# A four-layer RWKV and graph-conv network on one core: the first pair's sums on VectorE, the last layer norm ahead of a gelu, the last conv in another order of chunks

## The chip, the core and the metric

The kernel runs on one core of a Trainium2 chip. A core has TensorE (PE, matmuls into PSUM; PEld is its weight load), VectorE (DVE), ScalarE (ACT), GpSimd (POOL) and SyncE (SP, which here only issues DMAs). Each engine works through its own instruction queue in order; semaphores tie the queues together. The metric is the device time of one execution in microseconds (us), lower is better.

## What is computed

The input `x` is 16 images of 192 channels by 56 x 56. Three layers mix along the 3136 pixels with a two-way RWKV scan, a fourth is a graph conv. Each adds to its input, and each normalises its input first over groups of 6 channels and all pixels:

```python
xs = tokens(_gn(x))                       # layers 0 to 2; _gn: group norm, 32 groups
k, v, r = xs @ Wk.T, xs @ Wv.T, xs @ Wr.T
h = sigmoid(r) * 0.5 * (wkv_scan(k, v) + flip(wkv_scan(flip(k), flip(v))))
h = (h - mean(h)) * rsqrt(var(h) + eps) * ln_g + ln_b     # layer norm over channels
x = x + h @ Wo.T

g = _gn(x)                                # layer 3
x_j = max(roll(g, 2, rows), roll(g, -2, rows), roll(g, 2, cols), roll(g, -2, cols), g) - g
y = conv_w @ concat(g, x_j) + conv_b      # then batch norm
x = x + gelu(y)
```

## The kernel before

The images are worked two at a time, so there are eight *pairs*. A pair's 192 channels of two images fill three tiles of 128 partitions (`ORDER` = 0, 2, 1; tile 1 holds the upper 64 channels of both). The pixels are cut into `NL` = 7 *chunks* of `L` = 448. A *run* is one layer of one pair (`l` = 0 to 2 the scans, `l` = 3 the conv). A run's forward scan goes over chunks 0 to 6 (`"A"` units), its backward scan, gate, layer norm and output over chunks 6 to 0 (`"B"` units); a conv run has one `"C"` unit per chunk. `"Z"` units only load a pair's input so that its sums and squares can be counted.

The instructions of each engine are laid down by hand, in the order in which the Python code calls them, inside `manual_schedule`. Two streams of pairs interleave: while one pair is in its backward scan, the other is in a forward scan or a conv. A list `steps` pairs them up. Its first seven steps are the forward scan of pair 0 alone. Its last steps are: the backward scan of pair 7's third layer beside the conv of pair 6, the last conv chunk of pair 6 alone (`forward_c`), an empty step (`neither`), and the conv of pair 7, chunks 0 to 6, alone (`forward_c`).

The work around the change:

- **Statistics.** `chunk_stats` (L734, L735) takes a sum (Identity with accumulation) and a sum of squares per tile and chunk on ScalarE. For pair 0 all seven chunks are counted at the very start (L1708, L1709); at the same time the layer parameters are prepared outside the hand-made order (`layer_params`), and a scheduler mixes the two on each queue.
- **Group norm.** `norm_sums` (L740), `norm_var` (L749 to L765) and `norm_fold` (L777 to L784, L770) turn the sums into a scale that is folded into the layer's weights. They are called one part at a time through `gap()`. A group's mean rides as an extra column (`mean_column`, L765) behind chunk 0. The run's weights are loaded by `begin_later`, once the last chunk's new statistics are taken (`b_stats`).
- **Layer norm of a B unit.** After `b_mix` (L1031 to L1033, GpSimd) come `b_squares` (L1040, ScalarE), `b_sums` (L1047, L1049, TensorE), `b_rs1` to `b_rs3` (L1055, L1059, L1063, L1065), `b_spread` (L1071), `b_scale` (L1076), `b_out` (ops) and `b_x` (L1089 and the store to `xd`). `late` notes how far a unit has come. In the empty step `finish` brings the last units through.
- **Conv of a chunk.** `c_product` half 0 multiplies x (TensorE, "cv<-x"); `c_rows` (L1114 to L1116) and `c_columns` (L1125 to L1129) form the maxima on VectorE, from the chunk and two rows of its neighbours on each side, the *ring* `m<-xd`; `c_product` half 1 multiplies the maxima ("cv<-m"); `c_gelu` (L1150) reads PSUM on ScalarE; `c_add` (L1159) adds x on GpSimd for all three tiles at once; `store` (L1178 to L1181) issues four DMAs one step later.
- **Last of all**, outside the hand-made order, L1755 to L1759 reduce the accumulated checks to a flag, which decides whether a general version of the whole network is run after this one.

Of the kernel before, what the change touches and what calls it, by code (L numbers as in the profile page):

```python
# [473 lines left out]
def fast_path(ctx: ExitStack, tc: tile.TileContext, flag, x, wproj, wfold, wcfold, wconst, wgroup, sums, picks, vecs, out):  # L474
# [63 lines left out]
    def column(j):  # L538
        return slice(j % 2, j % 2 + 1)
# [172 lines left out]
    class Run:  # L712
        def __init__(self, pr, l, stats, src=None, first=None):
            self.pr, self.l, self.stats, self.src = pr, l, stats, src
            self.xa, self.xb, self.xz = {}, {}, {}
            if first is not None:
                self.xa[0] = first
            self.begun, self.before = False, None
            self.bias, self.ps = {}, {}
            self.ek, self.ekv, self.h, self.den, self.sg, self.rs = {}, {}, {}, {}, {}, {}  # L720
            self.m, self.ml, self.q, self.p = {}, {}, {}, {}
            self.done = set()
# [23 lines left out]
    def norm_var(run):  # L746
        m = run.ps["g"][:, 0:6].rearrange("p (j s) -> p j s", s=2)
        nm = run.nm = stile("nm")
        V.tensor_scalar(nm, m[:, :, 0:1], -1.0 / T, None, ALU.mult)  # L749
        m2 = stile("m2")  # L750
        V.tensor_mul(m2, nm, nm)
        var = run.var = stile("var")
        V.scalar_tensor_tensor(var, m[:, :, 1:2], 1.0 / T, m2, ALU.mult, ALU.subtract)
        release(run.ps.pop("g"))
        V.tensor_scalar(var, var, EPS, None, ALU.add)
        rstd = run.rstd = stile("rstd")
        S.activation(rstd, var, AF.Ln)
        S.activation(rstd, rstd, AF.Exp, scale=-0.5)
        run.chk = small.tile([P, NCHK], F32, tag="chk", name=name("chk"))
        mean_check = run.chk[:, 3 * NL + 9 : NCHK].rearrange("p (j o) -> p j o", o=1)  # L760
        V.scalar_tensor_tensor(mean_check, var, -MEAN_MAX, m2, ALU.mult, ALU.add)
        mean_column(run, run.xa[0])

    def mean_column(run, s):
        V.tensor_copy(s.full[:, :, L : L + 1], run.nm)  # L765
# [44 lines left out]
    def load_weights(run):  # L810
        kv = wpool.tile([P, 2, FCOLS], F32, tag="kv", name=name("wkv"))
        if run.l == NLAYERS:
            nc.sync.dma_start(kv, wcfold)
            run.weights = kv, None
        else:
            nc.sync.dma_start(kv, wfold[run.l, :, 0:2, :])
            r = wpool.tile([P, 1, FCOLS], F32, tag="r", name=name("wr"))
            nc.sync.dma_start(r, wfold[run.l, :, 2:3, :])
            run.weights = kv, r
        load_ahead(("C" if run.l == NLAYERS else "A", run, 0))  # L820

    def gap(eng=V):
        if norms:
# [11 lines left out]
    def load_ahead(unit):  # L835

        if unit is None:
            return
        kind, run, c = unit
        chunks = {"A": run.xa, "C": run.xa, "B": run.xb, "Z": run.xz}[kind]  # L840
        if c not in chunks and (kind, c) != ("B", NL - 1):
            chunks[c] = load_chunk(run, c)
        if kind == "C" and c not in run.xb:
# [264 lines left out]
    def c_rows(run, c):  # L1108
        xt, m = run.xa[c].t, run.xb.pop(c)
        run.m[c] = m  # L1110
        E = L - SHIFT
        if c == 0:
            mean_column(run, m)
        V.tensor_max(m.t[:, :, SHIFT:E], xt[:, :, 0 : E - SHIFT], xt[:, :, 2 * SHIFT : L])  # L1114
        V.tensor_max(m.t[:, :, 0:SHIFT], m.t[:, :, 0:SHIFT], xt[:, :, SHIFT : 2 * SHIFT])
        V.tensor_max(m.t[:, :, E:L], xt[:, :, E - SHIFT : E], m.t[:, :, E:L])  # L1116

    def c_columns(run, c):
# [9 lines left out]
        V.tensor_max(ml.t, ml.t, xt)  # L1128
        V.tensor_max(m, m, ml.t)  # L1129

    def c_product(run, c, half):
        n = L + 1 if c == 0 else L
        if half == 0:
            run.ps["c"] = banks("cv")
        s = (run.xa if half == 0 else run.m)[c]
        project(run.ps["c"], run.w[half], lambda rows, j: s.full[rows, j, 0:n], n, half == 0, half == 1)
        if half == 1:
            run.m.pop(c).give()

    def c_gelu(run, c, more):  # L1140
        g, ps = run.ml[c], run.ps["c"]
        if c == 0:
            run.bias["c"] = stile("cvb")
            for j in ORDER:
                V.tensor_scalar(
                    run.bias["c"][:, j, :], ps[j][:, L : L + 1], conv_inv[:, column(j)], conv_bias[:, column(j)],
                    ALU.mult, ALU.add,
                )
        for j in ORDER:
            S.activation(  # L1150
                g.t[:, j, :], ps[j][:, 0:L], AF.Gelu, bias=run.bias["c"][:, j, :], scale=conv_inv[:, column(j)]
            )
            release(ps[j])
        if not more:
            S.preload_act_table_set(TABLES)
# [9 lines left out]
    def c_end(run, c, more):  # L1165
        c_gelu(run, c, more)
        c_add(run, c)


    stores = []  # L1170
# [23 lines left out]
    for pr in range(npairs):  # L1194
        runs = [Run(pr, 0, None)]
        for l in range(NLAYERS):
            runs[-1].follow = Run(pr, l + 1, None)
            runs[-1].follow.before = runs[-1]
            runs[-1].dst = [dram.tile([P, 3, L], F32, tag=f"x{pr}_{l}_{c}", name=name("xd")) for c in range(NL)]
            runs.append(runs[-1].follow)  # L1200
        chains.append(runs)

# [9 lines left out]
    while ready[turn] is not None:  # L1212
        run, other = ready[turn], 1 - turn
        units = []
        ready[other] = None
        while todo[other]:
            r = todo[other].pop(0)
            units += front(r)
            if r.l < NLAYERS:
                ready[other] = r  # L1220
                break
        if len(units) > NL:

            units[NL - 1], units[NL] = units[NL], units[NL - 1]
        steps.append([("B", run, NL - 1), None, []])
        for c in reversed(range(NL - 1)):
            steps.append([("B", run, c), units.pop(0) if units else None, []])
        steps += [[None, u, []] for u in units]
        if len(streams) == 1 or ready[other] is None:

            units = []
            while todo[turn]:
                r = todo[turn].pop(0)
                units += front(r)
                if r.l < NLAYERS:
                    ready[turn] = r
                    break
            else:
                ready[turn] = None
            steps += [[None, None, []]] + [[None, u, []] for u in units]  # L1240
        else:
            turn = other
# [358 lines left out]
            keys(nkeys)  # L1601
            exp_keys(nkeys)

    def forward_c(a, nback, nfront):
        h = of_stage(0.5)
        load_ahead(nback)
        ahead = nfront is not None and nfront[1].begun
# [2 lines left out]
        if h and ahead and nfront[0] == "A":  # L1610
            c_rows(*a)
            b_rs2(*h)
            b_rs3(*h)
            sum_up(1)
            c_columns(*a)
            store()
            b_spread(*h)
            keys(nfront)
            exp_keys(nfront)
            b_scale(*h)  # L1620
            a_q(*nfront[1:])
            a_save(*nfront[1:])
            a_values(*nfront[1:])
            b_out(*h)
            late[h] = 2
            convs.extend(((a, 0), (a, 1)))
            return
        c_product(*a, 0)
        c_rows(*a)
        c_columns(*a)  # L1630
        store()
        if h:
            deviation_rest(h)
# [6 lines left out]
        if h:  # L1640
            b_out(*h)
            late[h] = 2
        c_end(*a, nfront is not None and nfront[0] == "C")
        if not ahead:
            sum_up()
            gap()
# [44 lines left out]
    def neither(nback, nfront):  # L1691
# [8 lines left out]
        keys(nfront)  # L1700
        exp_keys(nfront)

    with tc.manual_schedule(engines={PE.engine, V.engine, S.engine, G.engine, nc.sync.engine}):
        S.preload_act_table_set(TABLES)
        first = chains[0][0]
        for c in range(NL):
            load_ahead(("Z", first, c))
        for c in range(NL):  # L1708
            count([(first, c, j) for j in ORDER], 3)  # L1709
        for i, (b, f, z) in enumerate(steps):  # L1710
            nback, nfront, _ = steps[i + 1] if i + 1 < len(steps) else (None, None, None)
            for run in starts.get(i, ()):
# [28 lines left out]
            elif f and f[0] == "A":  # L1741
                forward_a(f[1:], nback, nfront, nkeys, z)
            elif f:
                forward_c(f[1:], nback, nfront)
            elif b:
                backward_alone(b[1:], nback, nfront)
            else:
# [6 lines left out]
    least = small.tile([P, 1], F32, tag="p2", name="fleast")  # L1754
    V.tensor_reduce(least, ok, mybir.AxisListType.X, ALU.min)  # L1755
    ps = bank("psok")

    PE.matmul(ps[0:32, 0:1], ones[:, 0, :], least, start=True, stop=True)
    V.tensor_scalar(flag, ps[0:1, 0:1], (P - 0.5) / C, None, ALU.is_lt)  # L1759


def kernel(tc: tile.TileContext, x, wproj, wconv, wconst, ones, vecs, wfold, wcfold, wgroup, sums, picks, out):
# [89 lines left out]
```

## Time and profile before

| what | value |
|---|---|
| median of 3 runs | 5207.93 us (5204.0 to 5208.27) |
| the profiled execution | 5220.16 us |
| span of its trace | 5218.2 us, 51856 instructions |
| granted TensorE clock, mean | 0.935 |
| q1, all loads and stores | 477.59 MB, 28.5% of 16 DMA engines' span |

In the profile, times are from the start of the span. A page line gives line, engine, operation, output <- input, count, busy time, mean ns of one, and idle time before it with what ended it. A timeline row gives start, duration, engine, line, operation and, in brackets, how long the engine had been idle and what released it. PE, DVE, ACT and POOL are the engines above; SPq is SyncE's DMA queue.

### The profile page before, as it was taken

Reading aid. Unit: us, or ns where it says so; the run is one execution under the profiler, and the core shown is the slowest. Engines: PE = TensorE matmul, PEld = TensorE weight load, DVE = VectorE, ACT = ScalarE, POOL = GpSimd, SP = SyncE. Lnnn points to the kernel's source line nnn. Section 1 sums busy time; section 2 is a strip of 40 time slices with the busy share of each in tenths; the row PEclk is TensorE's granted clock in tenths of the full one; section 3 lists DMA queues with packets and bytes.
Section 4 is the critical chain, followed back from the end, with each engine's and each line's share of the span. In section 5 each row is a group of like instructions: output and inputs, shape, how many; then the busy total and the mean of one; then the engine's idle time right before and its main releaser. Section 6 shows DMA issues by size and latency. Waiting matters only on the chain. (4 is left out here: it accounts for less than half of the span.)

```text
span 5218.2 us, 51856 instructions
## 1 busy us (share of the span) xinstructions
PE 4733.3 (91%) x15542; PEld 1498.8 (29%) x15542; DVE 4750.5 (91%) x6271; ACT 3684.6 (71%) x7163; POOL 2889.2 (55%) x2251
## 2 busy tenths in 40 slices
PE   7899998989899999998989999999898999999897
PEld 3222222223232222222323222222232322222222
DVE  6999999998989999999898999999889899999995
ACT  6777787776566777787656678777756667777772
POOL 1665665554545656565454556556545455666562
PEclk8999999999899999999989999999998999999998
DMA  5222222233232222223233223222333322222233
GB/s 154 69 82 87 90 86 89 85 110 97 90 116 72 87 90 93 82 90 122 93 93 101 84 75 100 88 85 87 128 93 101 93 74 77 72 84 77 80 104 120
DMA packets 314274, 482.47 MB, mean 92 GB/s; under 512 B 66432, under 2 KB 306688, under 8 KB 313984
## 3 DMA queue, kind: packets, MB, share of 16 engines
q1 hardware_dynamic: 312832, 477.59, 28.5%
q8 instruction: 126, 2.06, 0.2%
q10 hardware_dynamic: 1152, 1.48, 0.1%
q14 instruction: 164, 1.34, 0.1%
HBM read 324.83 MB, written 154.14 MB: 92 GB/s over the span
## 5 line engine op out<-in xcount | busy, mean ns | idle before, releaser
L875 DVE TENSOR_TENSOR_SCAN q<-fdecays,ek 128x449 f32<-128x449 f32 (+1 forms) x1008 | 1023.4, 1068 | 28.0 <-ACT ek L920 25.4
L875 DVE TENSOR_TENSOR_SCAN p<-fdecays,ekv 128x449 f32<-128x449 f32 (+1 forms) x1008 | 1020.3, 1065 | 0.6
L982 POOL TENSOR_TENSOR p<-p,q 128x1344 f32<-128x1344 f32 x168 | 512.0, 3047 | 830.3 <-ACT q L978 546.9
L1031 POOL TENSOR_TENSOR ekv<-ekv,ek 128x448 f32<-128x448 f32 x504 | 602.7, 1196 | 456.1 <-ACT ek L978 385.3
L1033 POOL TENSOR_TENSOR p<-p,sg 128x448 f32<-128x448 f32 x504 | 638.0, 1266 | 57.2 <-ACT ek L884 12.7
L1032 POOL TENSOR_TENSOR p<-p,ekv 128x448 f32<-128x448 f32 x504 | 606.1, 1203 | 39.5
L1040 ACT ACTIVATE ek<-p 128x448 f32<-128x448 f32 x504 | 286.4, 572 | 309.4 <-POOL p L1033 308.9
L886 POOL COPY ekv<-p 128x3 f32<-128x3 f32 x282 | 233.1, 827 | 488.0 <-DVE p L875 457.2
L1076 DVE TENSOR_TENSOR p<-p,rsb 128x448 f32<-128x448 f32 x504 | 282.4, 613 | 194.5 <-PE rsb L1071 194.4
L920 ACT ACTIVATE ek<-k,k 128x448 f32<-128x448 f32 x504 | 297.2, 632 | 225.3 <-PE k L601 179.2
L735 ACT ACTIVATE fjunk<-x 128x448 f32<-128x448 f32 x672 | 387.7, 577 | 40.1 <-DVE x L1089 13.4
L1071 PE MATMUL rsb<-rs,fpicks 32*128 32x448 f32 (+1 forms) x1008 | 359.2, 629 | 42.4 <-ACT rs L1065 42.4
L1159 POOL TENSOR_TENSOR ml<-ml,x 128x1344 f32<-128x1344 f32 x56 | 178.9, 3194 | 391.8 <-ACT ml L1150 391.8
L890 DVE SCALAR_TENSOR_TENSOR ek<-ek,fcc,q 128x896 f32<-128x896 f32 x336 | 379.1, 1167 | 0.0
L890 DVE SCALAR_TENSOR_TENSOR q<-ek,fcc,q 128x896 f32<-128x896 f32 x336 | 359.2, 1109 | 6.3 <-ACT cvb L954 4.6
L1089 DVE SCALAR_TENSOR_TENSOR x<-ops,fwob,x 128x448 f32<-128x448 f32 x504 | 314.2, 670 | 46.7 <-PE ops L601 26.6
L734 ACT ACTIVATE fjunk<-x 128x448 f32<-128x448 f32 x600 | 342.5, 571 | 11.4
L996 ACT ACTIVATE sg<-r,r 128x448 f32<-128x448 f32 x504 | 313.0, 627 | 33.5 <-PE r L607 20.7
L890 DVE SCALAR_TENSOR_TENSOR ekv<-ekv,fcc,p 128x896 f32<-128x896 f32 x336 | 330.1, 1022 | 0.0
L940 DVE SCALAR_TENSOR_TENSOR ekv<-v,v,ek 128x448 f32<-128x448 f32 x504 | 312.5, 672 | 16.6 <-PE v L601 8.0
L975 ACT ACTIVATE q<-q 128x1344 f32<-128x1344 f32 x168 | 221.5, 1318 | 125.5 <-DVE q L890 101.3
L890 DVE SCALAR_TENSOR_TENSOR p<-ekv,fcc,p 128x896 f32<-128x896 f32 x336 | 295.3, 919 | 6.5 <-POOL ekv L886 1.7
(235 smaller groups left out, 11546.4 us busy)
## 6 DMA issues: line engine op xcount, KB each, us to landing
x<-xd SPq DMA_DIRECT2D x240, 672.0 KB, 5.3
xd<-x SPq DMA_DIRECT2D x168, 672.0 KB, 3.9
x<-in_x_dram SPq DMA_DIRECT2D x320, 224.0 KB, 4.3
x<-in_x_dram SPq DMA_DIRECT2D x320, 112.0 KB, 4.2
out_dram<-ml SPq DMA_DIRECT2D x112, 224.0 KB, 2.3
m<-xd SPq DMA_DIRECT2D x112, 168.0 KB, 5.1
wkv<-in_wfold_dram SPq DMA_DIRECT2D x24, 640.0 KB, 5.6
out_dram<-ml SPq DMA_DIRECT2D x112, 112.0 KB, 2.3
```

What stands on the lines that cost most here:

```text
L734: S.activation(junk, xt[:, j, :], AF.Identity, accum_out=stats[:, 0, j, c : c + 1])
L735: S.activation(junk, xt[:, j, :], AF.Square, accum_out=stats[:, 1, j, c : c + 1])
L875: V.tensor_tensor_scan(out, dec[:, column(j)].to_broadcast([P, L if first else L + 1]), e, 0.0, ALU.mult, ALU.add)
L890: by_channel(lambda js, i: V.scalar_tensor_tensor(dst.t[:, js, :], e.t[:, js, :], cc[:, i : i + 1], state.t[:, js, :], ALU.mult, ALU.add))
L940: V.scalar_tensor_tensor(e.t[:, j, :], ps[j][:, 0:L], b[:, j, :], run.ek[c].t[:, j, :], ALU.add, ALU.mult)
L982: G.tensor_mul(run.h[c].t, run.h[c].t, den.t)
L996: S.activation(sg.t[:, j, :], ps[j][:, 0:L], AF.Exp, bias=b[:, j, :], scale=-1.0, accum_out=run.chk[:, at : at + 1])
L1031: G.tensor_mul(y.t[:, j, :], y.t[:, j, :], den.t[:, j, :])
L1032: G.tensor_add(h.t[:, j, :], h.t[:, j, :], y.t[:, j, :])
L1033: G.tensor_mul(h.t[:, j, :], h.t[:, j, :], sg.t[:, j, :])
L1071: PE.matmul(ps[j][:, :L], pick[rows, j, :], rs[rows, :], start=True, stop=True)
L1089: V.scalar_tensor_tensor(xj, ps[j][:, 0:L], wob[:, column(j)], xj, ALU.add, ALU.add, accum_out=run.new[:, 0, j, c : c + 1] if c == 0 else ...
```

## The change

Five edits are made together.

1. *Pair 0's sums.* The seven calls of `count` at the start are replaced. Per chunk, one VectorE reduction takes the sums of all three tiles; ScalarE takes only the squares (`chunk_stats(..., True)`).
2. *The last layer norm.* In the step of pair 6's last conv chunk, `forward_c` takes a new branch when only pair 7's conv is left (`final`). It runs the layer norm and output of pair 7's last unit there, with its squares first on ScalarE; the statistics of the two units before come after the deviation; the second half of the conv, the gelu and the add of pair 6's last chunk come after that, with the calls of `gap` between.
3. *The order of the last conv.* Pair 7's chunks go 3, 4, 5, 2, 6, 1, 0; the mean column goes to chunk 3 (`c0`). The maxima of chunks 3 and 4 are formed inside the new branch, and their loads are issued there.
4. *The end of the last chunk.* `c_end_in_parts` takes gelu, add (on VectorE) and stores tile by tile.
5. *The flag.* Its reduction moves ahead of that, inside the hand-made order.

```diff
@@ first pair's statistics
+        first.stats = input_stats()
         for c in range(NL):
-            count([(first, c, j) for j in ORDER], 3)
+            xs = first.xz.pop(c)
+            V.tensor_reduce(first.stats[:, 0, :, c : c + 1], xs.t, mybir.AxisListType.X, ALU.add)
+            chunk_stats(first.stats, xs.t, c, True)
+            xs.give()
@@ steps
+            if units[0][0] == "C":
+                last = units[0][1]
+                last.c0 = 3
+                units = [("C", last, c) for c in (3, 4, 5, 2, 6, 1, 0)]
@@ def norm_var(run):
-        mean_column(run, run.xa[0])
+        mean_column(run, run.xa[run.c0])
+        if run.c0 in run.m:
+            mean_column(run, run.m[run.c0])
@@ new
+    def maxima(run, c):
+        if c not in run.ml:
+            c_rows(run, c)
+            c_columns(run, c)
+
+    def c_end_in_parts(run, c):
+        g, ps, xs = run.ml.pop(c), run.ps["c"], run.xa.pop(c)
...
+        for j in ORDER:
+            S.activation(
+                g.t[:, j, :], ps[j][:, 0:L], AF.Gelu, bias=run.bias["c"][:, j, :], scale=conv_inv[:, column(j)]
+            )
+            release(ps[j])
+            V.tensor_add(g.t[:, j, :], g.t[:, j, :], xs.t[:, j, :])
+            if j == 1:
+                nc.sync.dma_start(out[b0, P:C, cols], g.t[LO, 1, :])
+                nc.sync.dma_start(out[b1, P:C, cols], g.t[HI, 1, :])
+            else:
+                nc.sync.dma_start(out[(b0, b1)[j // 2], 0:P, cols], g.t[:, j, :])
@@ def forward_c(a, nback, nfront, final):
+        l0, l2 = of_stage(0), of_stage(2)
+        if l0 and final:
+            r3, r4 = (u[1:] for u in final[:2])
+            load_ahead(final[0])
+            b_squares(*l0)
+            c_product(*a, 0)
+            c_rows(*a)
+            c_columns(*a)
+            store()
+            b_sums(*l0)
+            load_ahead(final[1])
+            if l2:
+                add(l2)
+            b_rs1(*l0)
+            b_rs2(*l0)
+            b_rs3(*l0)
+            b_spread(*l0)
+            sum_up()
+            maxima(*r3)
+            b_scale(*l0)
+            b_out(*l0)
+            c_rows(*r4)
+            add(l0)
+            sum_up()
+            c_product(*a, 1)
+            gap()
+            gap()
+            c_columns(*r4)
+            gap()
+            gap()
+            c_gelu(*a, True)
+            c_add(*a)
+            return
         c_product(*a, 0)
-        c_rows(*a)
-        c_columns(*a)
+        maxima(*a)
...
-        c_end(*a, nfront is not None and nfront[0] == "C")
+        if nfront is None:
+            flag_up()
+            c_end_in_parts(*a)
+            return
+        c_end(*a, nfront[0] == "C")
@@ new, in place of the same lines after the hand-made order
+    def flag_up():
+        least = small.tile([P, 1], F32, tag="p2", name="fleast")
+        V.tensor_reduce(least, ok, mybir.AxisListType.X, ALU.min)
+        ps = bank("psok")
+        PE.matmul(ps[0:32, 0:1], ones[:, 0, :], least, start=True, stop=True)
+        V.tensor_scalar(flag, ps[0:1, 0:1], (P - 0.5) / C, None, ALU.is_lt)
+        release(ps)
```

The rest of the diff gives a run's `src` when the chains are made, so that its chunks can be loaded before its norm, replaces `c == 0` by `c == run.c0` where the mean column is meant, and loads no ring for a chunk whose maxima exist. Chunk 0 of pair 7 stays in its tile from the layer before, as it did, and comes last now.

More of the change, by code (lines that the diff above doesn't have):

```diff
@@ L717, in __init__ @@
                 self.xa[0] = first
-            self.begun, self.before = False, None
+            self.begun, self.before, self.nm = False, None, None
+            self.c0 = 0
             self.bias, self.ps = {}, {}
@@ L819, in load_weights @@
             run.weights = kv, r
-        load_ahead(("C" if run.l == NLAYERS else "A", run, 0))
+        load_ahead(("C" if run.l == NLAYERS else "A", run, run.c0))
     def gap(eng=V):
@@ L842, in load_ahead @@
             chunks[c] = load_chunk(run, c)
-        if kind == "C" and c not in run.xb:
+        if kind == "C" and c not in run.xb and c not in run.m:
             ring = run.xb[c] = Slot("m")
@@ L1111, in c_rows @@
         E = L - SHIFT
-        if c == 0:
+        if c == run.c0 and run.nm is not None:
             mean_column(run, m)
@@ L1129, in c_columns @@
         V.tensor_max(m, m, ml.t)
+    def maxima(run, c):
+        if c not in run.ml:
+            c_rows(run, c)
+            c_columns(run, c)
     def c_product(run, c, half):
-        n = L + 1 if c == 0 else L
+        n = L + 1 if c == run.c0 else L
         if half == 0:
@@ L1141, in c_gelu @@
         g, ps = run.ml[c], run.ps["c"]
-        if c == 0:
+        if c == run.c0:
             run.bias["c"] = stile("cvb")
@@ L1167, in c_end @@
         c_add(run, c)
+    def c_end_in_parts(run, c):
+        g, ps, xs = run.ml.pop(c), run.ps["c"], run.xa.pop(c)
+        b0, b1 = 2 * run.pr, 2 * run.pr + 1
+        cols = slice(c * L, (c + 1) * L)
+        for j in ORDER:
[9 more added lines that the diff above has]
+                nc.sync.dma_start(out[(b0, b1)[j // 2], 0:P, cols], g.t[:, j, :])
+        g.give()
+        xs.give()
     stores = []
@@ L1199, in fast_path @@
             runs[-1].dst = [dram.tile([P, 3, L], F32, tag=f"x{pr}_{l}_{c}", name=name("xd")) for c in range(NL)]
+            runs[-1].follow.src = runs[-1].dst
             runs.append(runs[-1].follow)
@@ L1602, in forward_a, with forward_c @@
             exp_keys(nkeys)
-    def forward_c(a, nback, nfront):
+    def forward_c(a, nback, nfront, final):
         h = of_stage(0.5)
@@ L1707, in fast_path @@
             load_ahead(("Z", first, c))
+        first.stats = input_stats()
         for c in range(NL):
-            count([(first, c, j) for j in ORDER], 3)
+            xs = first.xz.pop(c)
+            V.tensor_reduce(first.stats[:, 0, :, c : c + 1], xs.t, mybir.AxisListType.X, ALU.add)
+            chunk_stats(first.stats, xs.t, c, True)
+            xs.give()
         for i, (b, f, z) in enumerate(steps):
@@ L1743, in fast_path @@
             elif f:
-                forward_c(f[1:], nback, nfront)
+                final = []
+                if all(b is None and u is not None and u[0] == "C" for b, u, _ in steps[i + 2 :]) and nfront is None:
+                    final = [u for _, u, _ in steps[i + 2 :]]
+                forward_c(f[1:], nback, nfront, final)
             elif b:
@@ L1751, in fast_path @@
         assert not late and not unsummed and not convs and not half
[L1754 to L1759, printed above, removed]
 def kernel(tc: tile.TileContext, x, wproj, wconv, wconst, ones, vecs, wfold, wcfold, wgroup, sums, picks, out):
```

## The prediction

> **What bounds the kernel now.** I read the page's busy table first, then the timelines of the first 60 us and the last 130 us, then the busy times of those stretches and, for two lines, the spread of single durations.
>
> ```profile
> PE 4733.3 (91%) x15542; PEld 1498.8 (29%) x15542; DVE 4750.5 (91%) x6271; ACT 3684.6 (71%) x7163; POOL 2889.2 (55%) x2251
> ```
>
> In the middle TensorE and VectorE are both busy 91% of the span. The listing of the changed program has the same instructions in the same order on every engine between the first pair's norm and the last norm, so only the two ends can move. Timeline of the start (start, duration, engine, line; idle before and releaser in brackets):
>
> ```profile
> 32.95 0.23 DVE L688 COPY fwo<-psctr 64x64 f32<-64x64 f32 x1
> 49.04 0.58 ACT L735 ACTIVATE fjunk<-x 128x448 f32<-128x448 f32 x1
> 49.52 0.19 ACT L735 ACTIVATION_READ_ACCUMULATOR fjunk<-x 128x1 f32 x1
> 49.74 0.20 DVE L740 TENSOR_REDUCE mv<-zstats 128x6 f32<-128x42 f32 x1 [16.56 <-ACT fjunk L735]
> ```
>
> ScalarE's chain of sums and squares ends last; VectorE idles 16.56 us behind it. Timeline of the end:
>
> ```profile
> 5087.77 2.33 POOL L1033 TENSOR_TENSOR p<-p,sg 128x448 f32<-128x448 f32 x1
> 5090.06 3.03 POOL L1159 TENSOR_TENSOR ml<-ml,x 128x1344 f32<-128x1344 f32 x1
> 5090.15 2.96 DVE L640 TENSOR_TENSOR fok<-fok,req 128x3 f32<-128x3 f32 x1
> 5106.84 1.49 ACT L1040 ACTIVATE ek<-p 128x448 f32<-128x448 f32 x3
> 5115.60 0.62 DVE L1076 TENSOR_TENSOR p<-p,rsb 128x448 f32<-128x448 f32 x1 [20.71 <-PE rsb L1071]
> 5130.49 0.82 DVE L783 TENSOR_TENSOR wkv<-wkv 128x640 f32<-128x640 f32 x1 [1.40 <-DMA wkv<-in_wcfold_dram]
> 5132.02 1.86 PE L598 MATMUL cv<-x,wkv 128*128 128x449 f32 x2 [5.00 <-ACT wkv L770]
> 5154.08 1.86 PE L598 MATMUL cv<-m,wkv 128*128 128x448 f32 x2 [5.53 <-DVE m L1129]
> 5202.57 1.02 PE L598 MATMUL cv<-m,wkv 128*128 128x448 f32 x2 [1.16 <-DVE m L1129]
> 5208.05 3.02 POOL L1159 TENSOR_TENSOR ml<-ml,x 128x1344 f32<-128x1344 f32 x1 [6.95 <-ACT ml L1150]
> 5212.72 0.58 SPq L1181 DMA_DIRECT2D out_dram<-ml  x1
> ```
>
> The last unit's layer norm has its input at 5090.10 (L1033), yet its squares (L1040) start at 5106.84, behind a gelu and twelve statistics passes. The conv then runs 5132.02 to 5207.07 on TensorE, waiting for maxima (L1129) twice, and a 3 us add on GpSimd stands before the last stores.
>
> ```profile
> 21.70:49.70 28.00, 9.89 (x29) 5.51 (x28) 3.60 (x19) 26.78 (x81) 0.00 (x0) 0.74 1.07 264
> 5090.10:5132.00 41.90, 22.98 (x74) 7.64 (x72) 12.06 (x30) 17.95 (x45) 6.01 (x2) 0.75 0.25 83
> 5132.00:5207.30 75.30, 68.59 (x198) 22.35 (x198) 62.51 (x104) 16.21 (x24) 20.81 (x6) 0.91 0.50 151
> ```
>
> Columns: stretch, length, busy PE, PEld, DVE, ACT, POOL, granted clock, DMA share, GB/s. ScalarE fills the first stretch; nobody fills the second; TensorE nearly fills the third.
>
> **Start: sums on VectorE.** Removed: 21 Identity passes with their read-outs, 0.70 us apart on ScalarE. 17 squares then stay behind the last layer parameter (about 24.8): 24.8 + 17 x 0.70 = 36.7. Added: seven reductions of 128x1344. The trace has none; the nearest row is L1128, 1344 two-input elements in 1.56 us. The Trainium skill speaks against the edit: "VectorE: DVE Perf Modes", Rules for kernel authors, calls `tensor_reduce` the slowest VectorE operation, one element per cycle, and says to consider restructuring. At its 0.96 GHz that is an estimate of 1.40 us bare, 9.8 us for seven against 10.9 us by the row. I take the row; even so it beats 3 x 0.70 on ScalarE and lies beside the squares.
>
> In VectorE's new order the first three reductions stand among parameter work (chunk 0 has landed by 2.42 + 5.3 = 7.7, chunks 1 and 2 by 12.9 and 16.3, before their turn). Behind them wait u-w, for which ScalarE waits, and the copies of `fwo`; those copies themselves wait for TensorE until about 28. The fourth reduction holds back the last copies to about 34.4; three more end at 34.4 + 4.7 = 39.1. So L740 comes at about 39.3 instead of 49.74: **-10.4 us**. Bounds: free reductions leave the squares (-12.9); at twice the row -4. Nothing later eats it: weights and chunk 0 are issued by 25.4, some 5.3 us from landing, and chunk 1 is needed 11 us after the next stretch starts, which VectorE fills (76.86 of 78 us).
>
> **End: the norm of the last unit.** New order: squares, then half a conv of pair 6's last chunk, sums, and so on.
>
> Squares end at 5090.10 + 0.57 = 5090.7 instead of 5108.33. The sums stand behind that half conv on TensorE (to 5091.97) and take 1.7 (as 5062.94 to 5064.65): 5093.7. From rs1 to the scale the old chain took 5111.09 to 5115.60 = 4.5: ready at 5098.3. But ahead of the scale on VectorE now stand b_x of the unit before (1.86, from 5089.1) and chunk 3's maxima (6.85, as 5153.94 to 5160.8), while GpSimd's add runs until 5093.1. The question is who is locked out:
>
> ```profile
> L1089 DVE SCALAR_TENSOR_TENSOR x<-ops,fwob,x x504: 646/672/687, 183.2 to 5123.7; 128x448 f32<-128x448 f32 x168
> L1128 DVE TENSOR_TENSOR ml<-ml,x x56: 1558/1559/4443, 1102.1 to 5196.6; 128x1344 f32<-128x1344 f32 x56
> ```
>
> (ns, minimum/median/maximum.) The maxima stretch, b_x never. The skill, "SBUF — State Buffer", Who interferes with whom, says why: two SBUF inputs contend with a GpSimd instruction that reads SBUF, one input does not. So b_x ends at 5091.0 and the maxima run 5093.1 to 5099.9. A rule of full blocking makes each add cost 3 us; the rows of the old run give 14.7 us lost in six adds, 2.45 each, which I use. The scale is 1.6 us late. Output product as before (6.4 us, slow clock) after the first scaled tile: ends T = 5106.9, not 5123.68. ScalarE's twelve passes (8.4 us from 5096.6) finish before it needs ScalarE again.
>
> From T to the conv's first matmul the old kernel took 8.3 us. Now TensorE does the other half of pair 6's conv first (4.5), so the group sums wait: 4.5 + 1.5; mean and variance 1.1; then chunk 4's column maxima (5.3) stand **ahead of the fold** on VectorE; small operations 0.8, L783 0.82, first fold 0.7. Sum 14.7, so the conv starts at X = 5121.6, **-10.4 us**. The weights (5.4 us in DMA, issued 1.4 after T) no longer end last; the columns do. Chunk 4's load, queued on SP behind pair 6's store (5093.1), lands by 5102 and is not late.
>
> **Conv.** Alone, TensorE needs 7 x 9.02 + 2.93 (its first half took 7.44 against 4.51 after the idle) = 66.1. Two maxima are done before X, which removes the 5.53 wait. The third chunk's load is late: SP holds it behind two stores, the first behind pair 6's gelu and add: fold end X + 1.1, table 1.3, gelu 2.0, add 3.05, stores 2.45 + 2.5, load 4.9 = X + 17.4. Five maxima, 34.3, and five adds in their way, 12.2, end at X + 63.9; half a product more gives X + 68.4 against 75.05: **-6.6 us**. Chunk 0 keeps its tile, so its load goes, hidden. The late gelu and table load lie under chunk 3's products (10 us).
>
> **Last stores.** Adds by tile on VectorE (about 0.62 each by L1125) wait behind the flag, which waits for TensorE (0.41 after the product): 0.41 + 1.9, two issues 1.0: 3.3 after the product, where the old last issue ended 6.2 after it. SP now reads the flag ahead of these stores with nothing to cover it; the trace does not time that read, bounds 0 and 1.5 us, nearer the register operations that are too short to list; I take 0.4. **-2.5 us**. Flag arithmetic alone is hidden under the last half product.
>
> **Sum.** -10.4 - 10.4 - 6.6 - 2.5 = -29.9. The profiled execution took 5220.16 (span 5218.2 plus 1.96 around it): 5190.3. It lies 12.2 above the median of the runs, 5207.93, from which the same amount gives **5178 us**.
>
> **Rivals.**
> - *VectorE becomes the conv's bound with colder restarts.* Each chunk waits about 1.5 us and TensorE restarts slowly (6.70 instead of 4.51 after 5154.08): five times 3.7 = 18.5 on 66.1, so the run is 84.6, 9.5 over the old one. Then -10.4 - 10.4 - 2.5 + 9.5 = -13.8: 5194. For it: VectorE needs 6.85 + 2.45 = 9.3 a chunk against 9.02. Against: the old run had one such restart. A milder form, half of it, gives 5186.
> - *The reductions are twice the row.* Start -4: 5184. Against: L740 takes 0.20 for 42 elements.
> - *Better.* Adds miss the maxima and TensorE sets the run (66.1): 5176; with the columns' 5.3 hidden as well, 5170.
> - *Slower.* The lock in the conv again, worse: with W us of waiting per chunk and a cold restart (2.2) each time, the change totals -21.4 + 5W. It is slower by 0.2% from W = 6.4, maxima of 15.4 us a chunk; 5.53 was seen once, but the longest maxima took 12.1 (two adds). At W = 7: 5222.
> - That the change does nothing is out: the new order shows 21 passes gone and the squares ahead.
>
> **Chances.** 0.2% (10.4 us) is about what a measurement of this kernel can tell. Forecast with the mild forms 0.72, its own range 5170 to 5186; cold restarts 0.08, of which 0.02 end within 0.2%; slow reductions 0.07; better 0.07; slower 0.03; other causes, such as another granted clock in the middle (0.92 to 0.96 by stretch), 0.03, mostly no change. So faster 0.92, same 0.05, slower 0.03. Bounds of the unknowns (start -4 to -13, end -13 to -26) give 5169 to 5191; with the spread of runs, 5167 to 5192.
>
> **What would show it.** Right: the first reduction of the sums at about 39; the last squares before 5092 less the start's gain; columns between variance and fold; the conv's run 66 to 70 us; the last store about 3.3 us after the last product. Wrong: VectorE reductions over 2 us, TensorE waiting for L1129's successor at every chunk, or idle time at the start moved to a load.

## The result and the profile after

The changed kernel took 5171.55 us in the median of four runs (5167.61 to 5175.38), beside 5207.7 for the kernel before: ratio 0.9932, 95% interval 0.9915 to 0.9949, or 36 us less. The forecast was 5178, range 5167 to 5192. The profiled execution is the fastest of the four, 5167.61 (span 5165.5). The profiled one of before was the slowest there was, so the two spans lie 52.7 us apart, which is more than the kernels differ. From the page of after, its busy times:

```profile
PE 4700.9 (91%) x15542; PEld 1488.9 (29%) x15542; DVE 4753.7 (92%) x6281; ACT 3667.0 (71%) x7118; POOL 2886.8 (56%) x2250
```

TensorE and VectorE share the lead as before; ScalarE has lost the 21 Identity passes. The timeline of the start, after (start, duration, engine, line; idle before and releaser in brackets):

```profile
28.07 0.23 DVE L688 COPY fwo<-psctr 64x64 f32<-64x64 f32 x1
28.33 4.47 DVE L1792 TENSOR_REDUCE zstats<-x 128x3 f32<-128x1344 f32 x3
33.67 0.58 ACT L737 ACTIVATE fjunk<-x 128x448 f32<-128x448 f32 x1
34.15 0.19 ACT L737 ACTIVATION_READ_ACCUMULATOR fjunk<-x 128x1 f32 x1
34.37 0.20 DVE L742 TENSOR_REDUCE mv<-zstats 128x6 f32<-128x42 f32 x1 [1.56 <-ACT fjunk L737]
```

The statistics reduction (L740 in the old numbering) comes at 34.37 instead of 49.74. In this execution the copies of `fwo` were done at 28.3, VectorE's last three reductions took 1.49 us each from one to the next, and ScalarE's squares ended last. The timeline of the end, after:

```profile
5051.94 2.34 POOL L1037 TENSOR_TENSOR p<-p,sg 128x448 f32<-128x448 f32 x1
5053.20 1.86 DVE L1093 SCALAR_TENSOR_TENSOR x<-ops,fwob,x 128x448 f32<-128x448 f32 x3
5054.24 3.06 POOL L1168 TENSOR_TENSOR ml<-ml,x 128x1344 f32<-128x1344 f32 x1
5054.31 0.58 ACT L1044 ACTIVATE ek<-p 128x448 f32<-128x448 f32 x1 [4.07 <-POOL p L1037]
5054.98 3.03 DVE L1118 TENSOR_TENSOR m<-x 128x672 f32<-128x672 f32 x1
5081.41 1.56 DVE L1133 TENSOR_TENSOR m<-m,ml 128x1344 f32<-128x1344 f32 x1
5082.89 0.15 DVE L781 TENSOR_TENSOR gt<-rstd 128x3 f32<-128x3 f32 x1
5085.07 1.86 PE L598 MATMUL cv<-x,wkv 128*128 128x449 f32 x2 [8.45 <-ACT wkv L774]
5112.43 1.86 PE L598 MATMUL cv<-m,wkv 128*128 128x448 f32 x2 [3.24 <-DVE m L1133]
5151.21 1.02 PE L598 MATMUL cv<-m,wkv 128*128 128x448 f32 x2 [1.18 <-DVE m L1133]
5155.97 0.14 DVE L1781 TENSOR_SCALAR flag<-psok 1x1 int32<-1x1 f32 x1 [4.72 <-PE psok L1780]
5157.05 0.81 SPq L1193 DMA_DIRECT2D out_dram<-ml  x2
5157.95 1.99 SPq L1190 DMA_DIRECT2D out_dram<-ml  x1
5160.00 0.58 SPq L1191 DMA_DIRECT2D out_dram<-ml  x1
```

Take the last mix's end (5054.28) as zero, as 5090.10 was in the old trace. The squares (L1044) start at once. The conv's first matmul waits 8.45 us, for the fold, which itself stands behind the column maxima that end with L1133 and are followed at once by the fold's small operations (L781). Inside the conv TensorE waits for maxima twice, for 3.24 us at the third chunk and for 1.18 us ahead of the last half product. The last issues stand at the bottom. Busy times of three stretches, after (stretch, length, busy PE, PEld, DVE, ACT, POOL, granted clock, DMA share, GB/s):

```profile
21.70:34.30 12.60, 4.99 (x23) 2.58 (x22) 9.40 (x28) 12.06 (x42) 0.23 (x1) 0.81 1.06 297
5054.28:5085.07 30.79, 19.99 (x72) 6.77 (x73) 23.02 (x56) 13.44 (x38) 3.02 (x1) 0.77 0.38 122
5085.07:5155.97 70.90, 66.45 (x198) 21.75 (x198) 49.07 (x76) 18.19 (x27) 24.19 (x7) 0.95 0.47 141
```

The stretch nobody filled, 41.90 us, is down to 30.79; VectorE works in 23.0 of it. The conv is 70.9, of which TensorE is busy 66.5. Stage by stage, in us:

| Stage | Before | After | Difference | Forecast |
|---|---|---|---|---|
| to the first statistics reduction | 49.74 | 34.37 | -15.4 | -10.4 |
| from there to the last mix | 5040.4 | 5019.9 | -20.5 | 0 |
| last mix to the conv's first matmul | 41.9 | 30.8 | -11.1 | -10.4 |
| conv on TensorE | 75.1 | 70.7 | -4.4 | -6.6 |
| last product to the end of the last issue | 6.2 | 4.8 | -1.4 | -2.5 |
| rest | 4.9 | 4.9 | 0 | 0 |

Two rows ask for an explanation: the start, and a middle of 5000 us that the change does not touch.

### The profile page after: what moved, and what is told of

It reads as the page before. It is cut to its first block, busy times and chain, and to the rows that moved or that the text cites. A ratio compares the mean times of both kernels' runs of the same rounds, so it can differ in the third digit from the quotient of the medians.

```text
span 5165.5 us, 51833 instructions
## 1 busy us (share of the span) xinstructions
PE 4700.9 (91%) x15542; PEld 1488.9 (29%) x15542; DVE 4753.7 (92%) x6281; ACT 3667.0 (71%) x7118; POOL 2886.8 (56%) x2250
## 5 line engine op out<-in xcount | busy, mean ns | idle before, releaser
L1044 ACT ACTIVATE ek<-p 128x448 f32<-128x448 f32 x504 | 285.7, 573 | 310.7 <-POOL p L1037 310.3
L737 ACT ACTIVATE fjunk<-x 128x448 f32<-128x448 f32 x672 | 387.6, 577 | 31.4 <-issue 5.6
L736 ACT ACTIVATE fjunk<-x 128x448 f32<-128x448 f32 x579 | 330.5, 571 | 10.8
```

Source lines behind the costliest of these rows:

```text
L736: S.activation(junk, xt[:, j, :], AF.Identity, accum_out=stats[:, 0, j, c : c + 1])
L737: S.activation(junk, xt[:, j, :], AF.Square, accum_out=stats[:, 1, j, c : c + 1])
```

## Experiments

All profiles are cut at the same marks. "Start" is the first statistics reduction, "middle" runs from it to the last mix, the other columns as above; "end" is everything behind the last mix. The clock is the granted one, a mean over the execution. Each ratio to the kernel before compares runs on one chip, not the same chip for all kernels.

| Kernel | Ratio, 95% interval | Start | Middle (clock) | To first matmul | Conv | Last issue | End |
|---|---|---|---|---|---|---|---|
| before | | 49.74 | 5040.4 (0.935) | 41.9 | 75.1 | 6.2 | 128.1 |
| changed | 0.9932, 0.9915 to 0.9949 | 34.37 | 5019.9 (0.943) | 30.8 | 70.7 | 4.8 | 111.2 |
| start alone | 0.9964, 0.9943 to 0.9986 | 38.30 | 5031.5 (0.941) | 41.9 | 75.2 | 7.6 | 129.4 |
| end alone | 0.9973, 0.9950 to 0.9996 | 49.09 | 5025.3 (0.939) | 30.8 | 71.4 | 4.2 | 111.2 |
| norm first, old chunks | 0.9938, 0.9916 to 0.9961 | 37.87 | 5014.9 (0.945) | 25.6 | 77.9 | 4.2 | 112.8 |
| columns behind fold | 0.9921, 0.9897 to 0.9944 | 34.54 | 5016.0 (0.945) | 26.0 | 69.5 | 4.8 | 105.5 |
| third load early | 0.9926, 0.9901 to 0.9950 | 39.00 | 5042.2 (0.939) | 31.0 | 66.3 | 4.7 | 107.1 |
| both moves | 0.9936, 0.9910 to 0.9961 | 37.20 | 5019.0 (0.945) | 26.1 | 67.1 | 4.9 | 103.0 |
| and adds on VectorE | 0.9926, 0.9897 to 0.9954 | 37.58 | 5029.2 (0.942) | 25.9 | 65.4 | 4.5 | 100.6 |
| and flag early | 0.9928, 0.9902 to 0.9955 | 39.04 | 5042.8 (0.939) | 26.1 | 65.7 | 4.3 | 101.0 |
| adds, two queues | 0.9938, 0.9916 to 0.9959 | 37.54 | 5040.6 (0.940) | 26.1 | 65.6 | 4.0 | 103.3 |
| two queues, added products | 0.9904, 0.9877 to 0.9931 | 34.25 | 5034.0 (0.938) | 26.1 | 65.6 | 3.9 | 101.1 |
| reductions twice | 0.9963, 0.9938 to 0.9988 | 48.39 | 5035.3 (0.940) | 31.0 | 71.6 | 4.5 | 112.3 |
| changed, again | 0.9943, 0.9917 to 0.9970 | 38.20 | 5030.9 (0.940) | 30.8 | 71.6 | 4.8 | 112.3 |

Where the code of a stage is the same, the columns behind the middle repeat within 1.4 us. The middle, the same work in all of them, spreads over 28 us and is long where the granted clock is low. So a change of some 5 us can't be seen in these times, but it can be read in its stage.

### The two halves, each alone

The kernel before with the sums as in the changed one:

```diff
+        first.stats = input_stats()
         for c in range(NL):
-            count([(first, c, j) for j in ORDER], 3)
+            xs = first.xz.pop(c)
+            V.tensor_reduce(first.stats[:, 0, :, c : c + 1], xs.t, mybir.AxisListType.X, ALU.add)
+            chunk_stats(first.stats, xs.t, c, True)
+            xs.give()
```

> The kernel before with one edit: the first pair's sums as seven reductions on VectorE, all else old. Theory (start and end are two separate gains, the middle only differs from run to run): the first statistics reduction of 128x42 comes at about 34.4 us instead of 49.7, nothing later changes, so about -15 us (ratio 0.997); the end from the last mix to the end of the span keeps its 128.1 us. Rival 1 (the start also shortens the middle, which was 20.5 us shorter in the changed kernel's trace): about -35. Rival 2 (the idle time only moves behind the start, to a load): less than -5.

The changed kernel with this part taken back:

```diff
-            V.tensor_reduce(first.stats[:, 0, :, c : c + 1], xs.t, mybir.AxisListType.X, ALU.add)
...
+            count([(first, c, j) for j in ORDER], 3)
```

> The changed kernel with the old start (sums on ScalarE). Theory: -11.1 to the conv's first matmul, -4.5 in the conv, -1.3 behind it, so about -17 us (ratio 0.9967), and with the start alone the two add up to about -32. The end from the last mix to the end of the span lasts 111 us as in the changed kernel. Rival (the middle's 20.5 us belong to the end's edits, for instance by another order of loads): about -37.

Measured: 0.9964 and 0.9973, which of 5205.6 us is -18.7 (-29.7 to -7.3) and -14.1 (-26.0 to -2.1). The sum, -33, is about the whole gain of 36. Both rivals that give one half the middle's 20 us as well (-35, -37) lie outside, and so does the one by which the idle time only moves (less than -5). In the traces the start alone saves 11.4 and leaves the end at 129.4; the end alone saves 16.8 (128.1 to 111.2) and leaves the start at 49.09. But 38.30 is not 34.4: the expectation took the start from one trace.

### Why the start comes at 34 or at 38

TensorE's timeline in the start, the changed kernel's first profile:

```profile
21.22 0.59 PE L605 MATMUL psctr<-cmat 128*128 128x192 f32 x2
```

and the same instruction in the changed kernel run again:

```profile
23.26 1.01 PE L605 MATMUL psctr<-cmat 128*128 128x192 f32 x2
```

The same pair of products takes 0.59 in one and 1.01 in the other. The busy times of the stretch from 19 to 24 us give 1.00 as the granted clock in both, but this tells nothing here: the trace's record of the clock has its first entry at 19.34 us in the one and at 47.80 in the other, and time without an entry is listed as 1.00. Of the ten profiles that have this start, two ran fast (34.37, 34.54) and eight slow: 37.20 to 39.04, mean 38.1 (the kernel with the added products, below, not counted). The old start doesn't care: slow in the profile of before, 49.74, fast in "end alone", 49.09, since ScalarE ends last there. Who ends last in the slow case was tried by making each reduction twice:

```diff
             V.tensor_reduce(first.stats[:, 0, :, c : c + 1], xs.t, mybir.AxisListType.X, ALU.add)
+            V.tensor_reduce(first.stats[:, 0, :, c : c + 1], xs.t, mybir.AxisListType.X, ALU.add)
```

> The changed kernel with each of the seven reductions of the start made twice. Theory (behind the parameter copies VectorE's reductions end last when TensorE is slow, and just ahead of ScalarE's squares when it is fast): three more of 1.5 us behind the last copies, the statistics reduction of 128x42 at 42 to 43.5 us (slow) or 38.5 to 39.5 (fast). Rival (ScalarE's squares end last and hide them): 37 to 39 (slow) or 34.4 (fast), as in the changed kernel.

The reduction came at 48.39. VectorE's timeline of that kernel:

```profile
32.69 0.23 DVE L688 COPY fwo<-psctr 64x64 f32<-64x64 f32 x1
32.95 1.55 DVE L1792 TENSOR_REDUCE zstats<-x 128x3 f32<-128x1344 f32 x1
...
46.73 1.55 DVE L1793 TENSOR_REDUCE zstats<-x 128x3 f32<-128x1344 f32 x1
48.39 0.20 DVE L742 TENSOR_REDUCE mv<-zstats 128x6 f32<-128x42 f32 x1
```

Ten reductions now stand behind the last copy, not the six that were expected: all seven new ones fell there. But nothing hides them, 48.39 - 37.54 (a kernel whose copies end at the same time) = 10.85 = 7 x 1.55. With a slow TensorE the reductions end last; the rival, ScalarE, is out. If TensorE is slow because it starts cold, work in its idle first 8 us should help: the Trainium skill, "TensorE: Matmul & The Clock Gate", Part 1: The HAM clock gate, gives some 3.4 us of sustained work as enough. Eleven products of a zeroed tile, whose result is used nowhere, on top of a version described below:

```diff
+    G.memset(junk, 0.0)
...
+    heat = bank("heat")
+    for _ in range(11):
+        PE.matmul(heat[:, 0:L], junk[:, 0:P], junk, start=True, stop=True)
+    release(heat)
```

> As the one with two queues, and eleven products of a zeroed tile on TensorE in its idle first 8 us; their result is used nowhere. Theory (in the start TensorE runs its 128x192 products at half speed in most executions, 1.01 us a pair against 0.59, because it begins cold; where it was fast the statistics reduction of 128x42 came at 34.4 to 34.5 and where it was slow at 37.2 to 39.0): TensorE is fast from about 5 us on, the pair takes 0.59 and the reduction comes at 34.5 or earlier. Rival 1 (it cools again during the one-column products from 8.4 to 15 us): pair 1.01, reduction at 37 to 39. Rival 2 (the added products run slowly and push the first real one from 8.4 to 11): 40 or more.

TensorE's timeline of that kernel at the start, first as one group, then asked for in the windows from 1.00 to 6.50 and from 6.52 to 12.20:

```profile
1.24 11.14 PE L579 MATMUL heat<-fjunk 128*128 128x448 f32 x22 [1.24 <-POOL feps L572]
1.24 5.50 PE L579 MATMUL heat<-fjunk 128*128 128x448 f32 x7 [1.24 <-POOL feps L572]
5.88 6.50 PE L579 MATMUL heat<-fjunk 128*128 128x448 f32 x16
```

A product is two of these matmuls. The group's mean, 1.01 us a product, hides two rates: up to 5.88 us the matmuls start 0.75 us apart, from 6.58 us on 0.38 apart (one of them stands in both windows). So TensorE did get fast, some 5.3 us after the first of them. Busy TensorE later in that kernel (stretch, length, busy PE, granted clock, DMA share, GB/s):

```profile
16.76:33.50 16.74, 16.30 (x60) 0.50 1.07 294
```

From 16.76 us on the granted clock is 0.50, and the first 128x192 pair, at 17.47, took 1.01. That is the first rival: TensorE cooled again during the one-column products. The second rival is out as far as it has the added products slow, though they did push the parameter work back, from 8.4 to 12.2 us. The reduction is early all the same, as the next lines show:

VectorE's timeline:

```profile
30.00 3.02 DVE L1807 TENSOR_REDUCE zstats<-x 128x3 f32<-128x1344 f32 x2
33.28 0.36 DVE L691 COPY fwo<-psctr 128x192 f32<-128x192 f32 x1 [0.27 <-PE psctr L613]
33.99 0.23 DVE L694 COPY fwo<-psctr 64x64 f32<-64x64 f32 x1
34.25 0.20 DVE L748 TENSOR_REDUCE mv<-zstats 128x6 f32<-128x42 f32 x1
```

It comes at 34.25, but not for the reason given. What helped is that the instructions outside the hand-made order were put down anew, and now no reduction stands behind the last copy. So the copies' end (34.2) is the bound, and the 4.5 us that the reductions add behind them depend on an order that nobody wrote.

What decides whether TensorE gets fast in the start without added products was not tested. The records of the clock hold a hint: its first entries lie whole multiples of 3.41 us apart. Counted back in such steps to the first 128x192 product, a step falls 0.2 to 0.5 us behind that product's start in the three profiles where a pair gets down to 0.59, and 1.0 to 3.3 us behind it in the ten where it stays at 1.01. That would fit a start that depends on where the steps happen to fall.

### What the new order of chunks is worth

The changed kernel with chunks 0 to 6 in the conv and without the maxima under the norm (not shown: one condition, by which the run's checks are gathered at chunk 5 and not 6):

```diff
-                last.c0 = 3
-                units = [("C", last, c) for c in (3, 4, 5, 2, 6, 1, 0)]
+                last.c0 = 0
...
-            load_ahead(final[0])
...
-            load_ahead(final[1])
...
-            maxima(*r3)
...
-            c_rows(*r4)
...
-            c_columns(*r4)
```

> The changed kernel with the last conv's chunks in the old order 0 to 6, so that no maxima can stand under the norm; the norm still goes ahead of the gelu and the statistics, start and tail as changed. Theory: without maxima ahead of the scale (1.6 us) and without columns ahead of the fold (5.3) the conv's first matmul comes 24 us after the last mix instead of 30.8; the conv waits for maxima as the old one did and runs 75 us instead of 70.6. Together 2 us shorter than the changed kernel: about -34 against the kernel before. Rival (the order of chunks is what pays at the end): the conv waits at more chunks, 80 us or more, and the kernel is over 3 us slower than the changed one.

The first matmul comes 5.2 us earlier, at 25.6 (24 was expected), and the conv takes 77.9 (75). TensorE waits five times in that kernel. Its timeline, the first four of them:

```profile
5078.35 1.87 PE L598 MATMUL cv<-x,wkv 128*128 128x449 f32 x2 [3.50 <-ACT wkv L774]
5087.58 1.02 PE L598 MATMUL cv<-m,wkv 128*128 128x449 f32 x2 [2.29 <-DVE m L1133]
5093.61 0.99 PE L598 MATMUL cv<-x,wkv 128*128 128x448 f32 x2 [1.45 <-DMA x<-xd]
5103.16 1.86 PE L598 MATMUL cv<-m,wkv 128*128 128x448 f32 x2 [5.01 <-DVE m L1133]
```

One wait is for a load. The end is 112.8, against 111.2 and 112.3 in the two profiles of the changed kernel, between the two expectations: the new order is worth 0.5 to 1.6 us as it stands, about what the two profiles differ by (1.1). What it saves in the conv it loses ahead of it, since the columns hold up the fold. The norm put first earns the rest. The next two runs take those losses back.

### Columns behind the fold, the third load early

```diff
             gap()
             gap()
-            c_columns(*r4)
             gap()
             gap()
+            c_columns(*r4)
```

> The changed kernel with one move: the column maxima of the second chunk (5.3 us on VectorE) stand behind the norm's variance and fold and no longer between them. Theory (the columns end last ahead of the fold): the conv's first matmul comes 4.9 us earlier, 26 us after the last mix, the conv keeps its 70.6, because the third chunk's load hangs on the gelu that follows the fold; about -5 against the changed kernel, -37 against the one before. Rival 1 (VectorE's sum of maxima sets the conv's end wherever they stand): the conv grows by the same 5 us, no gain. Rival 2 (the folded weights' load ends last): the first matmul gains under 2 us.

```diff
             c_columns(*r4)
             gap()
             gap()
+            load_ahead(final[2])
```

> The changed kernel with one move: the load of the third chunk of the last conv is issued while the sync queue stands idle ahead of the fold, not behind the previous pair's last stores. Theory (that late load makes the 3.24 us wait and the cold restart of 1.5 us behind it): no wait at the third chunk, run 66 us instead of 70.7, end from the last mix 106.5 instead of 111.2. Rival (VectorE, 9.3 us of maxima and stretched operations a chunk, sets the end of the run anyway): the wait moves to later chunks and the run stays above 69.

> Both moves together: columns behind the fold and the third chunk's load early. Theory (two separate waits): first matmul 26 us after the last mix, run 66, end from the last mix 102 instead of 111.2. Rival (VectorE is the bound once the load is not, since the columns then also stand in the conv's stretch): run 69 to 70, end 105 to 106, no better than columns alone (105.5).

Columns behind the fold: first matmul at 26.0 (-4.8), conv 69.5, end 105.5. The load early: wait gone, conv 66.3, end 107.1. Both: 26.1 and 67.1, end 103.0, which is 8.2 less than 111.2 where the single moves gave 5.7 and 4.1. They add up but for 1.6. The rivals, by which VectorE's sum of work sets the conv's end wherever the maxima stand, fall, though TensorE still waits for maxima: with the columns behind the fold three times (1.82, 1.10 and 0.85 us), with both moves once (1.45).

### Additions on VectorE, then the last stores

```diff
-    def c_add(run, c):
+    def c_add(run, c, eng=G):
         xs, g = run.xa.pop(c), run.ml.pop(c)
-        G.tensor_add(g.t, g.t, xs.t)
+        eng.tensor_add(g.t, g.t, xs.t)
...
         maxima(*a)
+        if pend:
+            c_add(*pend.pop(), V)
         store()
...
-        c_end(*a, nfront[0] == "C")
+        if a[0].c0:
+            c_gelu(*a, True)
+            pend.append(a)
+        else:
+            c_end(*a, nfront[0] == "C")
```

> Both moves, and the last pair's conv additions go from GpSimd (3.0 us each, during which a two-input operation of VectorE stretches to about 3) to VectorE, each behind the next chunk's maxima. Theory (a 128x1344 addition costs VectorE 1.56 us, and the GpSimd one costs it 2.4 by the stretch): no operation of VectorE over 2 us in the conv, VectorE needs 8.4 us a chunk against TensorE's 9.0, run 65.7 to 66.5 with no wait, end from the last mix 101.5. Rival (in VectorE's order the addition waits for the gelu and holds the next maxima up): waits at each second half, run 69 or more.

VectorE's groups in the last 80 us of that kernel (count | busy, mean ns | idle before):

```profile
L1170 DVE TENSOR_TENSOR ml<-ml,x 128x1344 f32<-128x1344 f32 x7 | 10.9, 1558 | 3.4 <-ACT ml L1159 3.4
L1133 DVE TENSOR_TENSOR m<-m,ml 128x1344 f32<-128x1344 f32 x6 | 9.4, 1560 | 0.2
L1118 DVE TENSOR_TENSOR m<-x 128x672 f32<-128x672 f32 x5 | 4.3, 853 | 0.0
```

and in the changed kernel's conv:

```profile
L1133 DVE TENSOR_TENSOR m<-m,ml 128x1344 f32<-128x1344 f32 x5 | 10.5, 2104 | 0.2
L1118 DVE TENSOR_TENSOR m<-x 128x672 f32<-128x672 f32 x5 | 7.1, 1423 | 6.5 <-DMA x<-xd 6.5
L639 DVE TENSOR_TENSOR req<-chk,flimit 128x3 f32<-128x3 f32 x1 | 3.0, 3000 | 0.0
```

The means of 1558 and 853 ns are those of operations without a GpSimd addition beside them; the 2104 and 1423 have stretched ones among them, and a 128x3 comparison took 3.0 us. So did a 128x16 maximum that fell beside an addition; the next one, behind the addition, took 0.16:

```profile
5106.05 3.05 DVE L1130 TENSOR_TENSOR ml<-x 128x16 f32<-128x16 f32 x1
5109.03 0.16 DVE L1131 TENSOR_TENSOR ml<-x 128x16 f32<-128x16 f32 x1
```

With the additions on VectorE TensorE has no wait left: conv 65.4, end 100.6. Next, the flag's arithmetic ahead of the last half product:

```diff
         maxima(*a)
+        if nfront is None:
+            flag_up()
...
         if nfront is None:
-            flag_up()
             c_end_in_parts(*a)
```

> As the one with additions on VectorE, and the flag's arithmetic stands ahead of the last half product, so that the last three additions and the sync queue's flag read do not wait for the last product. Theory: the last issue ends 2.7 us behind the last product instead of 4.8, end from the last mix 99.5; the half product starts 0.3 later for it. Rival (the last store's issue of 2.0 us, or the flag read, is late by itself): still 4.3 or more behind the last product.

And, apart from this, the middle tile's stores on ScalarE's queue:

```diff
-                nc.sync.dma_start(out[b0, P:C, cols], g.t[LO, 1, :])
-                nc.sync.dma_start(out[b1, P:C, cols], g.t[HI, 1, :])
+                nc.scalar.dma_start(out[b0, P:C, cols], g.t[LO, 1, :])
+                nc.scalar.dma_start(out[b1, P:C, cols], g.t[HI, 1, :])
```

> The version with additions on VectorE, and of the last four stores the two of the middle tile are issued by ScalarE, behind its last gelu, and not by the sync queue. Theory (the sync queue's issues, one of them 1.7 to 2.7 us long, end last): the last issue ends 3.2 us behind the last product instead of 4.5, end from the last mix 99.4. Rival (a store's issue is stretched wherever it stands, or ScalarE pays for its own issues): 4.3 or more.

With the flag early, the last issue ended 4.3 us behind the last product, not 2.7. The sync queue of that kernel:

```profile
5173.86 2.73 SPq L1195 DMA_DIRECT2D out_dram<-ml  x2
5176.69 0.52 SPq L1192 DMA_DIRECT2D out_dram<-ml  x1
5177.26 0.59 SPq L1193 DMA_DIRECT2D out_dram<-ml  x1
```

The issues start at once behind the second addition, but two of them take 2.73 where the changed kernel's took 0.81: the long issue moved from the third store to the first two. The rival holds. With two queues the sync queue's last issue ends 2.1 us behind the last product, but ScalarE's own issues (ACTq) end at 4.0:

```profile
5171.77 0.54 ACTq L1192 DMA_DIRECT2D out_dram<-ml  x1
5172.34 1.46 ACTq L1193 DMA_DIRECT2D out_dram<-ml  x1
```

One issue is long again, 1.46 us, so the result lies nearer to the rival's 4.3 than to the theory's 3.2. And the end grows from 100.6 to 103.3, because the span goes on for 7.7 us behind the last issue (5.6 with the added products) and not for 4.9. ScalarE's two stores landed 4.0 us behind their issue in the median (3.9 with the added products), where the sync queue's stores take 2.3; what else lengthens the end was not separated.

### The changed kernel again

> The changed kernel itself once more, beside the versions above on one chip. Theory: the end from the last mix lasts 111.2 us as in its first profile, while the stretch from the first statistics reduction to the last mix, whose instructions are the same in every version, takes anything from 5015 to 5043 with the granted clock of the execution (0.945 to 0.939); the start comes at 34.4 or at 37 to 39. Rival (the 5019.9 us of that stretch are a property of the changed kernel): 5018 to 5022 again at another clock.

The end is 112.3, its first matmul again at 30.8. The middle takes 5030.9 at a clock of 0.940, 11 us more than in the first profile. So the middle's 20.5 us are no property of the change.

### A version with a shorter start and end

By time the best was the one with two queues and added products: 5160.59, ratio 0.9904 (0.9877 to 0.9931), beside 5183.52 and 0.9943 (0.9917 to 0.9970) for the changed kernel on that chip. The intervals overlap. By stages, start and end are 34.25 + 101.1 = 135.4 against 38.2 + 112.3 = 150.5. With one queue the end is 100.6; that end with a start that has no reduction behind the copies was not run.

## Why the prediction was right

**Start, -10.4: right, and the profile of after misleads here.** The step had three reductions end last, behind copies done at 34.4. In the eight profiles with a slow TensorE the reduction comes at 37.2 to 39.0 (in the repeat at 38.2, behind copies that end at 33.6), so the gain is mostly 10.7 to 12.5. Two parts of the term were off: the copies' end, taken 0.8 too late, and the reduction, 1.49 from one to the next and not 1.56. So the row of L1128 gave the price, and the 1.40 estimated from the Trainium skill's "VectorE: DVE Perf Modes", Rules for kernel authors, is near it; but that rule's advice to restructure would, taken alone, have kept the old start. What the prediction did not have is the fast TensorE, with which the squares end last at 34.3.

**Norm, -10.4 to the first matmul: right.** Squares 0.6 behind the mix, as said; end of the output product at 16.4 (16.8 said); from there 14.4 (14.7 said), with the columns last. The run with the columns moved showed that step: 14.4 became 9.4. b_x took 1.86 for three beside a GpSimd addition, and the maxima's first operation, two inputs, 3.03: what the step took from the old rows and the Trainium skill's "SBUF — State Buffer", Who interferes with whom.

**Conv, -6.6: right in mechanism, too much by 2 to 3 us.** The third chunk landed at 17.4 behind the first matmul, as worked out. The term that failed is "2.45 each" for five additions in the maxima's way. From 5102.54 to the last maxima's end at 5151.15 are 48.6 us; 34.3 are plain, so five stretches cost 14.3, or 2.9 each: almost the whole 3.0 us of an addition. In the old trace six additions cost 14.7; here each of five fell on a two-input operation and held it. The bound without waits, 66.1, was met by the runs that took the waits away, 66.3 and 65.4.

**Last stores, -2.5: too much by 1.** "Two issues 1.0" was the wrong term: the two issues behind the third addition took 2.6 us (5157.95 to 5160.58), one of them 1.99, where the old kernel's last took 0.58. What the flag's read cost, taken at 0.4, can't be told apart here: the first store starts 0.4 behind the first addition (5156.65 to 5157.05), but the last two wait for the third addition.

**The sum.** -11.6 (mean of the slow starts), -11.1, -3.5 to -4.4, -1.4 make -27.6 to -28.5, beside -29.9 forecast and -36 between medians (interval -44 to -27). Too much in the conv and the stores (3.3 to 4.2) and too little in the start and the norm (1.9) cancel in part. The 8 us by which the medians differ more than the stages lie within what the middle does from run to run. So how near 5171.55 came to the forecast is partly luck; the stages are what bears it out.

Of the rivals, the cold restarts at every chunk did not come (one, as forecast), nor the slow reductions. The better cases, TensorE setting the run and the columns hidden, did not come with this change, but both exist: the two moves made them.

## What to carry to other kernels

Read a change of ten microseconds in a kernel of five thousand from stages between fixed marks, and take two profiles, since the middle and the start differ from one execution to the next by more than the parts of the change. When work is moved into a gap, ask what it now stands ahead of: the maxima under the norm gave back 5 us by standing before the fold, and a queue that held one load behind two stores gave back another 4. A row that merges many instructions gives their mean; ask for it in smaller windows before a rate is read from it. An addition on GpSimd may be dearer to VectorE (2.9 us of stretch) than the same addition done there (1.56).

## What the runs showed of the hardware

- TensorE's 128x192 products at the start took 1.01 us a pair in most executions and, from some 19 to 20 us on, 0.59 in three of fourteen. In one profile it was busy for 12.44 of the 13.00 us from 20 to 33 us, and the pairs still took 1.01. Eleven 128x448 products made it fast 5.3 us after the first (a matmul every 0.75 us, then every 0.38), and it was slow again (clock 0.50) at 16.76, 4.4 us after the last of them. The page on the clock gate named above expects a start that varies from run to run, which agrees, and full speed after some 3.4 us, which the added products nearly bear out and the pairs that stayed at 1.01 do not.
- A GpSimd addition of two SBUF tiles held a two-input VectorE operation beside it in each of five cases in the conv, however small: a 128x16 maximum took 3.05 us and a 128x3 comparison 3.00, against 0.16.
- In thirteen of fourteen profiles (not in that of before) one of the last four store issues took 1.3 to 2.2 us instead of 0.3 to 0.8, and it was another store when the order changed. Where ScalarE issued the last two stores, they landed 4.0 us behind their issue and not 2.3, and the span went on for 7.7 us behind the last issue and not 4.9.
